# Asking for the next attention head's queries and keys a step sooner, in the middle of another chain of transfers

## The chip, the cores and the metric

One core of one Trainium2 chip runs the whole program. The metric is the device time of one execution in microseconds, the median of several runs. The engines are named as in the profile: PE multiplies matrices (PEld is its loading of weights), DVE works on vectors, ACT applies functions, POOL is the general engine and SP only issues transfers. Each engine works through its own list of instructions in order and waits at semaphores for the others. A DMA issued by SP is an instruction in SP's list too: it takes time there, and if it has to wait for something, all that SP has to issue after it waits as well.

## The reference

The program is a network of two layers on an image tensor of 4 x 32 x 32 x 384 values. The change lies in the attention of the first layer, per image 1024 tokens and 12 heads of width 32:

```python
qkv = x.reshape(B, N, C) @ qkv_w.T
attn = jax.nn.softmax(jnp.einsum('bhnd,bhmd->bhnm', q, k) * scale, axis=-1)
...                      # each query joins a group; each group picks its 96 best keys
row = gw.sum(axis=-1)
col = mask.sum(axis=2)   # how many groups of this head picked a key
attn = attn * (row[..., :, None] * col[..., None, :])
attn = attn / (attn.sum(axis=2, keepdims=True) + 1e-08)
out = jnp.einsum('bhnm,bhmd->bhnd', attn, v)
return out.transpose(0, 2, 1, 3).reshape(B, H, W, NH * HD) @ proj_w.T
```

Two normalisations follow each other: the softmax divides by a sum over the keys, and the second one divides by a sum over the queries of what the first has left. So the exponentials of a head must be there for all keys, and their sum over keys must be known for each query, before the second sum can be taken. After the attention come a mixture of experts, a local attention and a last feed-forward layer, which the change leaves alone.

## The kernel before, in words

The attention runs over 48 heads (4 images of 12) in 192 steps, four steps for each head. A step handles a pair of key blocks, 256 keys against all 1024 queries. Three heads are under way at once, and the loop at L889 writes out by hand what each step does, for head n = step // 4 and pair u = step % 4:

- `scores` (L649): PE multiplies keys by queries into `ps_s`. Four groups of 32 rows work side by side, so queries and keys of the head have first to be copied from the layout of the whole image (`q`, `k`: one tile for four heads) into `q4` and `k4`, each with 4 x 32 partitions. The copies are eight DMAs of 64 KB (L636 and L637, a q and a k for each r), issued by SP in the constructor of `Head`. There are two buffers of each.
- `exps` (L659): ACT takes the exponential of `ps_s` into `e`, with 17 buffers.
- `out` (L667, into `ps_o`): PE multiplies values by the weighed exponentials of a pair eight steps back, that is of head n-2. It needs `wv` of that pair. In PE's list it stands right behind the scores of the step.
- `total` (L667, into `ps_z`): PE sums the exponentials of the step before over the keys.
- `gather`, at u = 0, for head n-1, whose sums are now complete: ACT copies them to `zr` (L681); SP writes them to a row in memory (`z_row`, L683), waits for that to land and reads them back spread over the partitions (`zz`, L685).
- `keep`, at u = 3, for head n-2: ACT copies the head's result to `po`, and four DMAs bring it into the place of the head's queries, two from SP (L740) and two that accumulate from POOL (L738).
- `share` (L711 to L718), seven steps behind the scores, so first at u = 3 for head n-1: DVE multiplies the exponentials by `rz`, the reciprocals of the sums repeated on all partitions, sums over the queries as it goes, and makes `wv` from the values.
- `spread`, at u = 1, for head n-1: DVE adds the two halves of `zz` (`zall`, L693) and takes the reciprocal `rr` (L695); SP writes it to a row (`r_row`, L697), waits for its landing, and reads the row back to all partitions (`rz`, L699, 512 KB).

At the end of step u = 1 the loop makes `Head(n + 1)` (L933), with the eight loads, for scores that come three steps later. In SP's list they stand behind `r_row` and `rz`.

Other transfers go by SP between these. In steps 4 to 75 each step writes a block of zeros to memory (`room`, L85, called at L924). For 16 steps of each image but the first, tiles of the image before are projected: every second step stores a finished tile (L787), and the step after it loads the next tile's residue into the same buffer, so that the load waits for the store (L764). The tokens of the next image are fetched by L221.

PE has spare room in a step, which a planner fills with work for the next image, so much per step (`goal`, `spent`). Each piece has a cost and may have a condition. One condition, at L536, holds the making of a new chunk of `q` and `k` back until the head that reads the old chunk last has been made: `len(heads) > NH * (b - 1) + 4 * c + 3`.

Of the kernel before, what the change touches and what calls it, by code (L numbers as in the profile page):

```python
# [10 lines left out]
FP = mybir.dt.float32  # L11
# [6 lines left out]
P = 128  # L18
B, IMG, C = 4, 32, 384
NTOK = IMG * IMG  # L20
NB = NTOK // P
# [155 lines left out]
def attention(net, outer, router, x, x1, unsafe, qkv_wT, gpT, proj_wT, proj_w, gate_w, gate_b):  # L177
# [15 lines left out]
    NHEAD = B * NH  # L193
# [8 lines left out]
    with ExitStack() as ctx:  # L202
# [6 lines left out]
        tiny = ctx.enter_context(tc.tile_pool(name="at_tiny", bufs=4))  # L209
# [106 lines left out]
        def cost(time):  # L316
            nonlocal spent
            spent += time
# [6 lines left out]
        reached, heads, projected, valued = set(), [], set(), set()  # L325

        def rows_of(t):
            return min(P, ROWS - P * t)

        def load(b, t):  # L330

            im = images[b]
            n = rows_of(t)

            parts, r = [], 0
            while r < n:
                c, o = divmod(P * t + r, GW)
                w = min(n - r, GW - o)
                parts.append((c, o, r, w))
                r += w  # L340
            left = work.tile([P, NTOK], FP, name="tk_left", tag="tk_left", bufs=2)
            for half in range(2):
                cols = slice(half * 512, half * 512 + 512)
                ps = psum()
                for c, o, r, w in parts:
                    nc.tensor.matmul(
                        ps[r : r + w, :], lhsT=qmbd[:, c, o : o + w], rhs=im["k"][c][:, cols],
                        start=True, stop=True,
                    )
                nc.scalar.copy(left[:n, cols], ps[:n, :])  # L350
            loaded.add((b, t))
            cost(1.8 * len(parts))
            return left
# [267 lines left out]
        class Head:  # L621
            def __init__(self, n):
                self.n, self.b, self.h = n, n // NH, n % NH
                self.c, self.j = self.h // 4, self.h % 4
                self.rows = slice(32 * self.j, 32 * self.j + 32)
                self.im = images[self.b]
                assert (self.b, self.c, "qk") in reached

                self.q4 = big.tile([P, 512], FP, name="q4", tag="q4", bufs=2)
                self.k4 = big.tile([P, 512], FP, name="k4", tag="k4", bufs=2)  # L630
                q = self.im["q"][self.c][self.rows, :]
                k = self.im["k"][self.c][self.rows, :].rearrange("p (a e t) -> p a e t", e=2, t=P)
                for r in range(4):
                    rows_ = slice(32 * r, 32 * r + 32)
                    odd, half = divmod(r, 2)
                    nc.sync.dma_start(out=self.q4[rows_, :], in_=q[:, 512 * half : 512 * half + 512])  # L636
                    nc.sync.dma_start(  # L637
                        out=self.k4[rows_, :].rearrange("p (a t) -> p a t", t=P), in_=k[:, :, odd, :]
                    )
                self.es = []  # L640
                self.s = tiny.tile([P, NB], FP, name="s", tag="s")

            def scores(self, u):
                self.ps = []
# [30 lines left out]
                    self.z = ps_z.tile([P, 512], FP, name="ps_z", tag="z")  # L675
                self.four(self.z, u, lambda odd: ones)

            def gather(self):

                zr = work.tile([P, 512], FP, name="zr", tag="zr", bufs=1)  # L680
                nc.scalar.copy(zr, self.z)  # L681
                there = rows.tile([4, 512], FP, name="z_row", tag="z_row")
                nc.sync.dma_start(out=there, in_=zr.rearrange("(j r) q -> j r q", r=32)[:, 0, :])  # L683
                self.zz = tiny.tile([P, 2, NB], FP, name="zz", tag="zz", bufs=2)
                nc.sync.dma_start(  # L685
                    out=self.zz,
                    in_=there.rearrange("j q -> (j q)").rearrange("(e p i) -> p e i", e=2, p=P),
                )
# [68 lines left out]
        def residue(b, t):  # L757
            if late:
                o = late[0].tile([P, C], FP, name="o", tag="o", bufs=2)
            else:  # L760
                o = few.tile([P, C], FP, name="o", tag="o", bufs=1)
            residues[b, t] = o
            r = b * NTOK + t * P
            nc.sync.dma_start(out=o, in_=x[r : r + P, :])  # L764

        def project(b, t):
            im = images[b]
            r = b * NTOK + t * P
            if t == 0:
                im["o"] = few.tile([P, NB, NE], FP, name="gate_o", tag="gate_o", bufs=1)  # L770
                im["mv"] = few.tile([P, NB, 2], FP, name="mv", tag="mv")
            o = residues.pop((b, t))
            cost(2.0)
            ps = psum()
            linear(
                ps[:, : C + NE], lambda k: images[b]["q"][k][:, t * P : (t + 1) * P],
                lambda k: wproj[:, k, :],
            )
            projected.add((b, t))

            def add():
                nc.vector.tensor_tensor(o, o, ps[:, :C], ALU.add)
                nc.vector.tensor_copy(im["o"][:, t, :], ps[:, C : C + NE])
                st = few.tile([P, 6], FP, name="o_st", tag="o_st")
                nc.vector.bn_stats(st, o)
                nc.vector.bn_aggr(im["mv"][:, t, :], st)
                nc.sync.dma_start(out=x1[r : r + P, :], in_=o)  # L787

            ends.append(add)
# [56 lines left out]
        def search():  # L846

            for one in list(searching):
                if next(one, 0) == 0:
                    searching.remove(one)  # L850

        def widen(step):

            nonlocal begun
            if len(searching) < 2 and begun < len(tiles) and step >= begun * TURN - 9 and ready(*tiles[begun]):
                searching.append(topk(*tiles[begun]))
                begun += 1
                next(searching[-1])

        def begin(step):  # L860
            now[0] = step
            for f in others.pop(step, []):
                f()

        def end():
            while ends:
                ends.pop(0)()
# [8 lines left out]
        for step in range(-AHEAD, 0):  # L876
# [8 lines left out]
                search()  # L885
            end()
        heads.append(Head(0))
        goal = spent
        for step in range(STEPS + OUT + 2):  # L889
            n, u = divmod(step, PAIRS)  # L890
            if n < NHEAD:
                heads[n].scores(u)
            if n < NHEAD:
                heads[n].exps()
            if 0 <= step - OUT < STEPS:
                heads[(step - OUT) // PAIRS].out((step - OUT) % PAIRS)
            if 0 <= step - 1 < STEPS:
                heads[(step - 1) // PAIRS].total((step - 1) % PAIRS)
            if u == 0 and 0 < n <= NHEAD:
                heads[n - 1].gather()  # L900
            if 0 <= step - OUT < STEPS:
                if (step - OUT) % PAIRS == PAIRS - 1:
                    heads[(step - OUT) // PAIRS].keep()
            b, i = divmod(step, PAIRS * NH)
            goal = min(goal + (RAMP if step < 12 else PACE), spent + MOST)
            begin(step)
            if step < 12:
                search()
                search()
            widen(step)  # L910
            o, t = i - OUT - 2, (i - OUT - 2) // 2
            if b and 0 <= o < 2 * NB and o % 2 == 0:
                project(b - 1, t)
            if b and 0 <= o + 1 < 2 * NB and o % 2:
                residue(b - 1, t + 1)
            if b and o > 2 * NB:
                next(routing[b - 1], None)
            if b < B:
                for t in {3: [0], 4: [1, 2], 5: [3], 6: [4], 7: [5, 6], 8: [7]}.get(i, []):
                    value(b, t)  # L920
            while spent < goal and prepared():
                pass
            if zeros and step >= 4:
                zeros.pop(0)()  # L924
            if 0 <= step - SHARE < STEPS:
                heads[(step - SHARE) // PAIRS].share((step - SHARE) % PAIRS)
            if u == 1 and 0 < n <= NHEAD:
                heads[n - 1].spread()
            search()
            end()  # L930
            search()
            if u == 1 and n + 1 < NHEAD:
                heads.append(Head(n + 1))  # L933
        residue(B - 1, 0)
        assert not ends and not others
        assert pending == [None, None] and begun == len(tiles) and not searching and not zeros
# [1529 lines left out]
```

## Time and profile before

| | us |
|---|---|
| median of three runs (2771.51 to 2787.73) | 2778.27 |
| the profiled execution | 2779.0 |
| its span, first to last instruction | 2776.9 |
| PE, DVE, ACT, POOL busy in the span | 2563.9, 1746.2, 1272.1, 414.5 |
| attention's stretch, 75 to 1225 us: PE busy | 1017.1 |
| the same stretch: DVE, ACT busy | 824.2, 791.7 |
| the stretches after it: 1225 to 1980, 1980 to 2690, 2690 to 2777: PE busy | 741.7, 680.4, 75.0 |
| SP, one ask each, median: q<-q, k<-k | 0.597, 0.632 |
| SP, one ask each, median: zz<-z_row, rz<-r_row | 0.372, 0.320 |

A row of the list of waits reads: the engine and line that waited, what it waited for, then the microseconds in total, how often, and the longest. In a timeline a row gives the start, the duration and the instruction, with equal neighbours merged (x8), and in brackets the idle time of the engine before it with what ended it. "SPq" is SP's list: its rows are asks of DMAs, not the transfers. When a transfer has landed is seen from what waits for it.

### The profile page before, as it was taken

How to read it: one execution, taken by the hardware profiler on the slowest of the kernel's cores; microseconds unless marked ns; L12 is line 12 of the kernel's file. 1: busy time of each engine (PE TensorE's matmuls, PEld its weight loads, DVE VectorE, ACT ScalarE, POOL GpSimd, SP SyncE). 2: the span in 40 equal slices, each digit the busy share in tenths (PEclk: the TensorE clock that was granted, in tenths of full speed). 3: DMA queues.
4: the chain of work that ended last, by engine and by line, in shares of the span. 5: the costliest groups of instructions: out<-in, count | busy, mean ns of one | idle time of the engine just before them, and what ended most of it. 6: DMA issues, size and time to landing. Idle time of an engine off the chain costs nothing. (4 is left out here: it accounts for less than half of the span.)

```text
span 2776.9 us, 40200 instructions
## 1 busy us (share of the span) xinstructions
PE 2563.9 (92%) x14667; PEld 1555.7 (56%) x14667; DVE 1746.2 (63%) x4490; ACT 1272.1 (46%) x2086; POOL 414.5 (15%) x501
## 2 busy tenths in 40 slices
PE   6879998989898999679999999999999998999988
PEld 3323332333332332137889999999999974555542
DVE  2367768777776778555635444455465457897962
ACT  3768776667676777421121211211211123445455
POOL 1000000020003000412221111222222111110000
PEclk9989999989998999779999999999999999999999
DMA  5133334322331233445475455556656626765532
GB/s 108 33 98 91 103 91 124 104 56 63 92 78 46 70 87 85 130 128 190 158 280 207 181 187 207 213 208 222 228 195 223 225 100 220 213 213 180 174 117 93
DMA packets 215807, 404.13 MB, mean 146 GB/s; under 512 B 83345, under 2 KB 176849, under 8 KB 202545
## 3 DMA queue, kind: packets, MB, share of 16 engines
q0 software_dynamic: 26960, 209.05, 21.9%
q1 hardware_dynamic: 178928, 181.52, 21.8%
q10 hardware_dynamic: 9712, 10.91, 1.3%
q8 instruction: 118, 1.93, 0.3%
q14 instruction: 89, 0.72, 0.1%
HBM read 304.34 MB, written 49.00 MB: 127 GB/s over the span
## 5 line engine op out<-in xcount | busy, mean ns | idle before, releaser
L1728 ACT ACTIVATE h<-ps_h,up 128x256 f32<-128x256 f32 (+1 forms) x420 | 194.9, 465 | 835.2 <-PE ps_h L1723 818.6
L1723 PE MATMUL ps_h<-xbT,up 128*128 128x256 f32 (+1 forms) x2520 | 531.2, 371 | 2.5 <-ACT h L1728 1.4
L1723 PEld LDWEIGHTS ps_h<-xbT,up 128*128 128x128 f32 x2520 | 462.4, 191 | 64.9 <-ACT h L1728 2.2
L711 DVE CUSTOM_DVE_ANT_0 e<-e,rz,inv 128x1024 f32<-128x1024 f32 x384 | 475.2, 1274 | 35.7 <-DMA rz<-r_row 35.7
L659 ACT ACTIVATE e<-ps_s,ten 128x1024 f32<-128x1024 f32 x384 | 407.6, 1107 | 96.5 <-PE ps_s L649 41.6
L649 PE MATMUL ps_s<-q,k 32*128 32x512 f32 x1536 | 291.3, 669 | 66.1 <-ACT e L659 32.7
L667 PE MATMUL ps_o<-e,wv 128*32 128x512 f32 x1536 | 229.0, 671 | 47.6 <-DVE wv L718 30.2
L738 POOL DMA_DIRECT2D q<-po x96 | 76.0, 874 | 977.9 <-DMA q<-po 651.1
L667 PE MATMUL ps_z<-e,rt_ones 128*32 128x512 f32 x1536 | 219.7, 646 | 0.0
L391 ACT ACTIVATE below<-tk_left,tk_bound 128x1024 bf16<-128x1024 f32 (+1 forms) x160 | 184.2, 1151 | 70.6 <-DVE tk_bound L397 60.1
L1767 PE MATMUL ps_y<-wsum,hsum 128*128 128x192 f32 x1116 | 197.1, 330 | 9.9 <-DVE hsum L1683 5.4
L649 PEld LDWEIGHTS ps_s<-q,k 32*128 32x128 f32 x1536 | 89.4, 191 | 203.2 <-issue 89.3
L1767 PEld LDWEIGHTS ps_y<-wsum,hsum 128*128 128x128 f32 x1116 | 183.3, 192 | 13.7 <-DVE y L1771 7.4
L1907 PE MATMUL ps_a<-wa,xnT 128*128 128x486 f32 x384 | 162.4, 572 | 1.8 <-ACT xnT L174 1.8
L1771 DVE TENSOR_TENSOR y<-ps_y,y 128x192 f32<-128x192 f32 x155 | 55.4, 357 | 167.8 <-PE ps_y L1767 162.0
L667 PEld LDWEIGHTS ps_o<-e,wv 128*32 128x32 f32 x1536 | 31.7, 112 | 209.0 <-issue 83.5
L306 PE MATMUL ps_t<-xnT,wqkv 128*128 128x512 f32 x288 | 136.9, 616 | 3.3 <-ACT xnT L488 2.6
L1567 POOL DMA_INDIRECT yt<-yg,index x64 | 78.0, 1218 | 358.8 <-DVE x L1870 164.7
L667 PEld LDWEIGHTS ps_z<-e,rt_ones 128*32 128x32 f32 x1536 | 52.8, 118 | 132.7 <-issue 129.7
L1767 PE MATMUL ps_y<-down,h 128*128 128x192 f32 x744 | 126.0, 326 | 0.0
L1767 PEld LDWEIGHTS ps_y<-down,h 128*128 128x128 f32 x744 | 122.6, 190 | 1.6
L1907 PEld LDWEIGHTS ps_a<-wa,xnT 128*128 128x128 f32 x384 | 71.2, 189 | 74.2 <-issue 70.2
(403 smaller groups left out, 3588.1 us busy)
## 6 DMA issues: line engine op xcount, KB each, us to landing
band<-room SPq DMA_DIRECT2D x32, 1560.0 KB
rz<-r_row SPq DMA_DIRECT2D x48, 512.0 KB
yg<-y SPq DMA_DIRECT2D x67, 192.0 KB
q<-q SPq DMA_DIRECT2D x192, 64.0 KB
k<-k SPq DMA_DIRECT2D x192, 64.0 KB
room<-none SPq DMA_DIRECT2D x64, 192.0 KB
x<-x SPq DMA_DIRECT2D x34, 192.0 KB
o<-in_x_dram SPq DMA_DIRECT2D x33, 192.0 KB
```

The lines of the kernel that those rows point to most:

```text
L306: nc.tensor.matmul(ps, lhsT=lhsT(k), rhs=rhs(k), start=k == 0, stop=k == KC - 1)
L391: nc.scalar.activation(junk[:n], left[:n], AF.Sign, bias=bound[:n], accum_out=over[:n])
L649: nc.tensor.matmul(ps[:, half * 512 : half * 512 + 512], lhsT=self.k4[r, u * P : (u + 1) * P], rhs=self.q4[r, :], start=True, stop=True,)
L659: nc.scalar.activation(e, ps, AF.Exp, bias=shift, scale=QK_SCALE)
L667: nc.tensor.matmul(ps[r : r + 32, :], lhsT=lhsT(odd), rhs=self.es[2 * u + odd][:, half * 512 : half * 512 + 512], start=u == 0, stop=u == ...
L711: nc.vector.tensor_tensor_reduce(self.es[m], self.es[m], self.rz, 1.0, self.im["inv"][:, m, self.h : self.h + 1], ALU.mult, ALU.add, self. ...
L738: nc.gpsimd.dma_start(out=there, in_=po[r : r + 32, :], accum_op=ALU.add)
L1567: self.nc.gpsimd.indirect_dma_start(out=y, out_offset=None, in_=self.net.yg[: first_row(self.complete(i // NB)), :], in_offset=bass.Indire ...
L1723: nc.tensor.matmul(ps, lhsT=up[:, o : o + P], rhs=xbT[:, k, :size], start=k == 0, stop=k == KC - 1,)
L1728: nc.scalar.activation(hs[f // 3][:, f % 3, :size], ps, AF.Gelu, bias=up[:, KC * HID + f : KC * HID + f + 1])
L1767: nc.tensor.matmul(ps, lhsT=left[f], rhs=right[:, f, :], start=f == 0, stop=f == HF - 1)
L1907: nc.tensor.matmul(pa[:, :HW_], lhsT=xnTs[i][:, k, :], rhs=wa[:, k, hh * HW_ : (hh + 1) * HW_], start=k == 0, stop=k == KC - 1,)
```

## The change

`Head`'s constructor only makes the tiles; a generator `load` issues the eight DMAs, stopping after each. The head is made at u = 0 of the head before it, not at the end of u = 1. `gather` is given the generator and takes three of the loads between the ask of `z_row` and that of `zz`; the other five follow right behind `zz`. Head 0 is loaded in one go before the loop, head 1 at step 0.

```diff
@@ class Head
+                self.es = []
+                self.s = tiny.tile([P, NB], FP, name="s", tag="s")
+
+            def load(self):
+
                 q = self.im["q"][self.c][self.rows, :]
...
                     nc.sync.dma_start(out=self.q4[rows_, :], in_=q[:, 512 * half : 512 * half + 512])
+                    yield
                     nc.sync.dma_start(
                         out=self.k4[rows_, :].rearrange("p (a t) -> p a t", t=P), in_=k[:, :, odd, :]
                     )
-                self.es = []
-                self.s = tiny.tile([P, NB], FP, name="s", tag="s")
+                    yield
...
-            def gather(self):
+            def gather(self, loads):
...
                 nc.sync.dma_start(out=there, in_=zr.rearrange("(j r) q -> j r q", r=32)[:, 0, :])
+                for _ in range(3):
+                    next(loads, None)
                 self.zz = tiny.tile([P, 2, NB], FP, name="zz", tag="zz", bufs=2)
@@ the loop over steps
         heads.append(Head(0))
+        for _ in heads[0].load():
+            pass
...
-            if u == 0 and 0 < n <= NHEAD:
-                heads[n - 1].gather()
+            if u == 0 and n <= NHEAD:
+                loads = iter(())
+                if n + 1 < NHEAD:
+                    heads.append(Head(n + 1))
+                    loads = heads[-1].load()
+                if n:
+                    heads[n - 1].gather(loads)
+                for _ in loads:
+                    pass
...
-            if u == 1 and n + 1 < NHEAD:
-                heads.append(Head(n + 1))
```

The transfers are the same in number, size and shape.

## The prediction

> **What bounds the kernel now.** I read the table of stretches first: attention, 75 to 1225 us, is the stage with a slack engine clock and idle matrix time (PE busy 1017.1 of 1150 us; the four shorter stretches each show it), and the diff touches nothing outside it. What the change can win or lose there has to come out of PE's 133 idle us, so next came the list of waits for that window. Three rows name the two things that share the sync queue: a head's loads (first two lines) and the row of reciprocals that DVE needs before it may weigh the exponentials (last two).
>
> ```profile
> PE ps_s L649 <- DMA q<-q: 11.7, 1, 11.7
> PE ps_s L649 <- DMA k<-k: 11.0, 10, 4.2
> PE ps_o L667 <- DVE wv L718: 30.2, 14, 5.2
> DVE e L711 <- DMA rz<-r_row: 35.7, 15, 13.2
> ```
>
> Then the order of the queue itself, from the timeline of SP after head 7's sums are ready (columns: start, duration, what):
>
> ```profile
> 281.24 0.55 SPq L683 DMA_DIRECT2D z_row<-zr  x1
> 282.98 0.38 SPq L685 DMA_DIRECT2D zz<-z_row  x1
> 283.40 1.24 SPq L85 DMA_DIRECT2D room<-none  x2
> 285.07 0.32 SPq L697 DMA_DIRECT2D r_row<-rr  x1
> 286.57 0.33 SPq L699 DMA_DIRECT2D rz<-r_row  x1
> 287.36 0.59 SPq L636 DMA_DIRECT2D q<-q  x1
> 287.99 0.66 SPq L637 DMA_DIRECT2D k<-k  x1
> ...
> 291.97 0.63 SPq L637 DMA_DIRECT2D k<-k  x1
> ```
>
> Each ask waits for the landing of the one before it: z_row to zz 1.74 us, zz to r_row 2.1 us (landing, an add, a reciprocal), r_row to rz 1.5 us. The last of head 9's eight loads is asked at 292.60, and head 9's first scores (DVE and PE timelines) need it:
>
> ```profile
> 290.40 1.27 DVE L711 CUSTOM_DVE_ANT_0 e<-e,rz,inv 128x1024 f32<-128x1024 f32 x1
> 293.12 0.22 DVE L718 TENSOR_TENSOR wv<-v,d 128x64 f32<-128x64 f32 x1
> ```
>
> ```profile
> 292.40 1.53 PE L649 MATMUL ps_s<-q,k 32*128 32x512 f32 x6
> 294.13 1.09 PE L649 MATMUL ps_s<-q,k 32*128 32x512 f32 x2 [0.21 <-DMA k<-k]
> 295.16 1.06 PE L667 MATMUL ps_o<-e,wv 128*32 128x512 f32 x8
> ```
>
> The scores stretch to 2.8 us where other heads show 1.14. But ps_o of head 7 comes right behind them, and its weights wv were done only at 293.34. So PE has two late guests at this step, and they are nearly equally late. That is the heart of the case.
>
> **What the change gains.** For every head I compared the first ps_o behind its first scores with the earliest it could start with the loads already there: PE's previous end and ACT's last two exponentials, and wv of the head two back. The difference (loads' lateness not covered by wv) is 1.7 us at head 9, 0.7 at 10, 2.1 at 18, 2.3 at 28, 1.8 at 30, 0.9 at 42, 1.0 at 43, 1.6 at 47; elsewhere the loads end over 1 us ahead or something else binds. Sum: 12.1 us, if rz comes no later than now. The new asks begin right behind z_row, some 5 us sooner, and no first scores would wait for them: that part I take as certain but for head 47 (see below).
>
> **What the change costs: the sum's own asks.** The loads take SP's time: 0.60 us for q, 0.63 for k by the median of their rows, 0.66 from one ask to the next (287.36 to 291.97 is seven of them). Three now stand between z_row and zz, where 1.74−0.59 = 1.15 us were idle; five between zz and r_row, where some 1.7 to 1.8 were. Zz: 0.58 + 3×0.66 = 2.6 us behind z_row, not 1.74, so 0.8 later. Loads end at 2.6 + 0.42 + 5×0.66 = 6.3. A plain head's r_row then goes at 6.3, not 3.9: 2.4 us late, and rz, which nothing shortens, as late. Where the two room writes lie between (heads 4 to 10) they no longer fit in idle time: 6.3 + 2×0.62 = 7.6, so 3.8 late. Where a finished tile is stored and the next residue loaded (L787, L764; heads 14, 16, 28, 38 to 41), the residue waits for the store's landing and r_row stands behind it: at head 38 that is 6.3 + 1.35 + 1.5 + 0.4 = 9.6, where the timeline has 5.4: 4.2 late. Where r_row waited anyway for DVE or ACT (heads 1, 2, 11, 15, 26, 29, 44: it went 6 to 14 us behind z_row) nothing is lost.
>
> What is queued behind: on DVE the add that waits for zz, then the first weighing (L711) of that head and all DVE work after it; on PE the ps_o that needs wv, and everything behind; ACT's second exponential of that step, whose buffer that ps_o frees. POOL's accumulating writes (L738) hang on the asks of L740 two steps on, by when SP has caught up: nothing. Keeping the queue clear at the end of the old step costs nothing either way.
>
> Rz's lateness reaches PE only past two covers: DVE was busy elsewhere when rz landed, and wv was ready before PE came. Per head (r_row late − DVE's cover − PE's cover, with the worst of the four pairs):
> Head 4: 3.8−0.5−0.4 = 2.9, of which 1.5 falls into an idle wait of PE's that follows (ACT's g): 1.4. Head 7: 3.8−0−1.3 = 2.5. Head 8: 3.2−0.3−0.8 = 2.1, swallowed by the 3.4 us wait for ACT's exponential that follows: 0. Head 14: 4.0−0.3−1.0 = 2.7. Head 16: 3.8−0.2−2.1 = 1.5 (its store also queues behind a 768 KB load). Head 28: 3.5−0.3−1.8 = 1.4. Head 38: 4.2−0.5−0.6 = 3.1, less a 0.7 wait: 2.4. Head 39: 3.0−0.3−1.3 = 1.4. Head 40: 3.0−0.4−0.9 = 1.7. All others have cover: in plain heads 18 to 25, 30 to 37 and 42 to 43 the 2.4 us is met by 1.9 to 12 us of DVE and PE slack. Sum: 15.0 us lost.
>
> Now the gains again, since ps_o takes the later of its two guests. Heads 9, 10, 18, 30 and 42 have as second guest wv of heads 7, 8, 16, 28 and 40, which are in that list: their losses are counted from a ps_o that already waited for loads, so their gains are gone. Head 28 keeps 2.2 (head 26's r_row is hardly late), head 43 nothing (41 is 0.3 to 0.9 late), head 47 0.3: 2.5 us kept.
>
> **Net:** +15.0 − 2.5 = +12.5 us.
>
> **Unknown costs, from both sides.** (1) Zz and r_row now stand in the DMA rings behind loads. Behind nothing, zz lands in 1.65 us, r_row in 1.4. The Trainium skill (DMA: Bandwidth & Descriptors, Queues, rings and completion order) says that each DMA engine takes descriptors in ring order, which speaks against this change; what it costs depends on whether a backlog stands there. Head 9's last load fed a matmul 1.5 us after its ask had ended, as fast as the 8 KB zz: no backlog at one 64 KB load per 0.66 us. I take 0; by the rule with half a us on each, the same sum over heads rises by 5, with a full us by 12. Below nothing: rz of heads 46 and 47, with no loads asked behind, landed 3.3 to 3.4 us after its ask against about 3.55 for the rest; 0.2 on eight paying heads is −1.6.
> (2) The same page (Issuing engines are not separate DMA queues) says that the time a sequencer takes to start a DMA is usually small beside the DMA. By that rule the eight asks would push nothing and the sum would be −12.1. The row says 0.60 to 0.63 each, back to back, and z_row to zz is only 1.74: I go by the row. At 0.50 per ask the losses would halve, at 0.35 they vanish.
> (3) The planner asks `len(heads) >` before it makes a chunk of the next image's q and k; heads are listed two steps sooner. The copies into q and k show four chunks held by exactly this (steps 26, 42, 90, 138); they move two steps forward. The matmuls are the same; a step with them is 5.7 us, one without 3.3 to 4.0, of which PE works 3.3. Between −0.7×2×4 = −5 and, if they meet a DVE-bound step, +5. I take 0.
> (4) Head 47's loads and r_row meet the first expert weights: r_row took 10.3 us to land there. Loads asked sooner get ahead of part of that traffic, but r_row falls behind them: −2 to +3, taken as −0.3.
> Moving `es` and `s` in the constructor issues nothing: 0. Head 1's loads are asked at step 0 on an idle queue: 0.
>
> **The sum.** The profiled execution took 2779.0 us (span 2776.9 and 2.1 around it), 0.7 over the median of 2778.27. 2779.0 + 12.5 = 2791.5, against the median 2790.8: I say 2791.
>
> **Rivals.**
> *Late sums, as above*: 2784 to 2799, 47%. For it: ask times and the order of the queue, both measured. Against: each cover is one execution's.
> *Loads win* (faster): PE's wait for loads at its first scores goes, and rz comes in time. It decides from the point where r_row is under about 1 us late in the storing and room-writing heads, that is if an ask costs under 0.45 us or DVE is usually busy past rz's landing. Then 2779.0−12.1 = 2767; 18%. For it: 22.7 us of PE waits carry the loads' names. Against: 11.7 of these are one event at head 47 where DVE waited 13.2 for rz at the same time.
> *They cancel*, or the early scores let ACT run ahead so that PE catches up behind a late ps_o: within 5 of 2779; 17%.
> *Sums later still*: ring backlog of half to one us, or paying heads among those I covered: 12.5 + 5 to 12 and a few more heads, 2797 to 2810; 18%.
>
> The runs shown spread over 16 us, so about 0.5% (14 us) is what a measurement here can tell from no change. Faster than 2764: 10% (half of the second). Slower than 2792: nearly half of the first and all of the last, 42%. Same: 48%. For 8 in 10 the range goes from the second's middle to within the last: 2767 to 2806.
>
> **What would show it.** Right: in SP's timeline zz about 2.6 us behind z_row, r_row 6.3 to 9.6; no rows "PE ps_s L649 <- DMA"; "DVE e L711 <- DMA rz" up from 35.7 to over 55 us, "ps_o L667 <- wv" up by 10 or more, and zall's wait up. Wrong: asks at 0.35 us; r_row at 4 to 5; or rz late with no more wait of PE for wv, its cover then being larger than this trace has it.

## The result, and the profile after

The changed kernel takes 2818.52 us (median of six runs, 2812.01 to 2826.27); the kernel before, run beside it, 2777.74. The ratio is 1.0163, 95% interval 1.014 to 1.0186: 40.8 us slower, where the prediction said 12.5. The direction was right, the size was not, and 2818 lies above the range of 2767 to 2806.

The list of waits of the changed kernel over its attention (75 to 1272 us; the largest rows of VectorE and TensorE that bear on the change, some rows between them left out; columns: microseconds in all, times, longest) answers to the one before:

```profile
DVE e L718 <- DMA rz<-r_row: 75.9, 34, 5.6
DVE zall L700 <- DMA zz<-z_row: 71.2, 29, 17.2
PE ps_o L672 <- DVE wv L725: 50.2, 20, 11.4
PE ps_s L654 <- ACT e L664: 36.5, 26, 4.2
PE ps_o L672 <- DVE tk_parts L395: 36.3, 11, 8.2
...
PE ps_t L487 <- DVE gate_o L790: 8.2, 5, 3.0
```

The kernel before has for three of these, beside the rows already shown:

```profile
DVE zall L693 <- DMA zz<-z_row: 35.4, 19, 4.1
PE ps_o L667 <- DVE tk_parts L395: 13.7, 6, 3.9
PE ps_t L487 <- DVE gate_o L783: 2.3, 3, 1.3
```

In the change there is no row of scores that wait for a DMA any more: the loads are in time everywhere. VectorE's wait for rz has more than doubled (35.7 before), and so has its wait for zz. Two rows are the wait for the weights wv at the output sums: the one that says so (30.2 before), and the one put down to tk_parts, an operation that starts on VectorE right behind wv as wv ends. Together they went from 43.9 to 86.5 us. The last row is new in this size: matmuls between the steps wait for VectorE too.

SP's timeline of the changed kernel, first behind the sums of head 7 (the head of the prediction's timeline), then behind those of head 40, where a tile is stored and a residue loaded (columns: start, duration, what):

```profile
287.98 0.55 SPq L688 DMA_DIRECT2D z_row<-zr  x1
...
290.61 0.52 SPq L692 DMA_DIRECT2D zz<-z_row  x1
...
293.83 0.63 SPq L643 DMA_DIRECT2D k<-k  x1
294.84 1.37 SPq L85 DMA_DIRECT2D room<-none  x2
296.31 0.55 SPq L704 DMA_DIRECT2D r_row<-rr  x1
298.12 0.33 SPq L706 DMA_DIRECT2D rz<-r_row  x1
...
1090.11 0.63 SPq L643 DMA_DIRECT2D k<-k  x1
1090.85 0.53 SPq L794 DMA_DIRECT2D x<-o  x1
1092.99 0.34 SPq L771 DMA_DIRECT2D o<-in_x_dram  x1
1093.42 0.38 SPq L704 DMA_DIRECT2D r_row<-rr  x1
1095.60 0.32 SPq L706 DMA_DIRECT2D rz<-r_row  x1
```

From z_row to rz it takes 10.1 us at head 7, where it was 5.3. What becomes of this at head 40 is seen on VectorE and TensorE:

```profile
1096.69 0.18 DVE L793 BATCH_NORM_AGGREGATE mv<-o_st 128x2 f32<-128x6 f32 x1
1099.78 1.28 DVE L718 CUSTOM_DVE_ANT_0 e<-e,rz,inv 128x1024 f32<-128x1024 f32 x1 [2.91 <-DMA rz<-r_row]
...
1102.52 0.22 DVE L725 TENSOR_TENSOR wv<-v,d 128x64 f32<-128x64 f32 x1
```

```profile
1095.68 1.61 PE L654 MATMUL ps_s<-q,k 32*128 32x512 f32 x8
1102.89 1.94 PE L672 MATMUL ps_o<-e,wv 128*32 128x512 f32 x8 [5.60 <-DVE tk_parts L395]
1104.57 1.92 PE L672 MATMUL ps_z<-e,rt_ones 128*32 128x512 f32 x8
...
1108.57 1.14 PE L654 MATMUL ps_s<-q,k 32*128 32x512 f32 x8
```

Rz lands 4.2 us after its ask, wv is ready 3 us behind that, and TensorE has stood 5.6 us. Then a second thing shows: ps_o and ps_z take 1.9 us each, where 1.07 and 1.04 are usual. The granted clock is 0.50 from 1101 to 1104 us and full again from 1107. My prediction had no such term, so a theory of the cause had to include it.

**Where the time is.** The kernel before and the change were profiled once more on one chip (e8 and e7 below), and each stretch from the first scores to the last ps_o was split: TensorE's idle time, its busy time, and of this half of what it was busy while the granted clock was 0.5.

| us | before (e8) | change (e7) |
|---|---|---|
| TensorE's work, counted at full clock | 943.1 | 935.7 |
| added by half clock | 77.2 | 88.6 |
| idle | 124.1 | 166.5 |
| of it ahead of ps_o / ps_s / ps_t | 57.2 / 47.6 / 18.9 | 95.1 / 39.9 / 29.2 |
| the stretch | 1144.3 | 1190.8 |

So +46.5 us is 42.4 of waits, 11.4 of clock and −7.4 of work. Both stretches hold the same 6470 matmuls, so the −7.4 says how exact the last two terms are: TensorE's busy time as a whole rose by only 4.0 us. All that follows the stretch takes about the same (1545 and 1552 us).

### The profile page after: what moved, and what is told of

Same layout as the page of the kernel before. It is cut to its first block, busy times and chain, and to the rows that moved or that the text cites. A ratio compares the mean times of both kernels' runs of the same rounds, so it can differ in the third digit from the quotient of the medians.

```text
span 2817.5 us, 40166 instructions
## 1 busy us (share of the span) xinstructions
PE 2572.7 (91%) x14667; PEld 1555.7 (55%) x14667; DVE 1747.8 (62%) x4490; ACT 1273.5 (45%) x2086; POOL 415.3 (15%) x501
## 5 line engine op out<-in xcount | busy, mean ns | idle before, releaser
L718 DVE CUSTOM_DVE_ANT_0 e<-e,rz,inv 128x1024 f32<-128x1024 f32 x384 | 475.8, 1276 | 76.2 <-DMA rz<-r_row 75.9
L672 PE MATMUL ps_o<-e,wv 128*32 128x512 f32 x1536 | 237.6, 695 | 96.2 <-DVE wv L725 50.2
L654 PE MATMUL ps_s<-q,k 32*128 32x512 f32 x1536 | 280.5, 671 | 37.6 <-ACT e L664 36.5
L672 PE MATMUL ps_z<-e,rt_ones 128*32 128x512 f32 x1536 | 228.8, 670 | 0.0
L1781 PEld LDWEIGHTS ps_y<-wsum,hsum 128*128 128x128 f32 x1116 | 183.4, 192 | 12.5 <-DVE hsum L1697 6.7
```

Of the source, the lines that this page charges most:

```text
L654: nc.tensor.matmul(ps[:, half * 512 : half * 512 + 512], lhsT=self.k4[r, u * P : (u + 1) * P], rhs=self.q4[r, :], start=True, stop=True,)
L672: nc.tensor.matmul(ps[r : r + 32, :], lhsT=lhsT(odd), rhs=self.es[2 * u + odd][:, half * 512 : half * 512 + 512], start=u == 0, stop=u == ...
L718: nc.vector.tensor_tensor_reduce(self.es[m], self.es[m], self.rz, 1.0, self.im["inv"][:, m, self.h : self.h + 1], ALU.mult, ALU.add, self. ...
L1781: nc.tensor.matmul(ps, lhsT=left[f], rhs=right[:, f, :], start=f == 0, stop=f == HF - 1)
```

## The experiments

My theory: the eight asks ahead of r_row make rz late, ps_o waits, and each wait costs up to double because the clock falls (row theory, with the clock theory as its second half). Rivals: the planner, which the new position of the heads' list makes move work (in the change's trace four makings of q and k come two steps sooner, into steps that hold a head's first ps_o), and traffic, that the loads themselves get in the way of the small transfers, whoever asks for them. The kernel before took 2751 to 2752 us beside some of the runs and 2776 to 2782 beside others (chip 8 gave both: 2775.7 beside e5 to e8, 2752.3 beside e13 to e15), for no reason that the record shows; so ratios to the kernel before, run side by side, are compared, and microseconds only between runs made side by side. "Landing" is the median, over heads 3 to 43, of the time from the end of zr to the end of the last 4 KB packet of rz: 9.4 to 9.5 us in the kernel before, 13.3 in the change.

**e7, e8: the change and the kernel before once more, e16: the change on another chip.** No edit.

> The change itself once more, so that the other runs have it, with a profile, on their chip: 1.5 to 1.8% above the kernel before. Against the run with the planner held (1.0154): if the planner's shift carries nothing, the ratio is between 1.012 and 1.019; if it carries a good part of the loss, 1.02 or more.

> The kernel before, unchanged, for a profile on the same chip as the others. Clock theory: its stretch with attention holds at least 35 us less at half clock than the same stretch of the change beside it. If the half clock is a thing of the chip and not of the waits: within 15 us of it.

> The change itself, to set beside the two runs that follow on the same chip: 1.0155 to 1.021 of the kernel before.

1.0155 (1.0113 to 1.0198) and 1.0164 (1.0144 to 1.0183): the result stands on other chips too. Half clock in the stretch was 189.9 us before and 226.1 in the change, 36 more.

**e1: the planner held.**

```diff
-                    (b == 0 or len(heads) > NH * (b - 1) + 4 * c + 3)
+                    (b == 0 or asked() > NH * (b - 1) + 4 * c + 3)
...
+        def asked():
+            n, u = divmod(now[0], PAIRS)
+            return len(heads) - (now[0] >= 0 and u < 2 and n + 1 < NHEAD)
```

> The change, but the condition that frees a query and key chunk for preparing counts the next head only from the third step of a head, as in the kernel before; the order of asks on SP stays that of the change. Row theory (the late reciprocal row makes the output sums wait, and the waits halve TensorE's clock): most of the +40.8 us stays, 2803 to 2820. Planner theory (preparing work moved by two steps carries the loss): 2780 to 2797.

1.0154 (1.0134 to 1.0175). The microseconds of the expectation don't apply here (2796 beside 2751), the ratio does: the whole loss is there with the planner as before. The planner's rival falls; what it moves changes where the waits stand (78.9 us ahead of the first ps_o of a head, 56 to 66 in the change's runs), not their sum.

**e2, e12: GpSimd asks, with the planner held and as in the change.**

```diff
             def load(self):
...
-                    nc.sync.dma_start(out=self.q4[rows_, :], in_=q[:, 512 * half : 512 * half + 512])
+                    nc.gpsimd.dma_start(out=self.q4[rows_, :], in_=q[:, 512 * half : 512 * half + 512])
...              # the same for k4
```

> As the run with the planner held, but the eight loads of a head are asked by GpSimd in place of SP, so that they are as early as in the change and nothing stands between the finished head's asks. Row theory: the row rz lands as in the kernel before, and the loads' gain is left: 2765 to 2778. Traffic theory (the eight transfers themselves, early, get in the way of the small ones, whoever asks): 2795 to 2815.

> The change with nothing altered but the queue of the eight loads: GpSimd asks them, the planner is as in the change. Row theory: within 0.3% of the run with GpSimd's asks and the planner held (0.9948), so 0.992 to 0.998. If the planner's shift costs something that the late row hid: 1.000 or more.

0.9948 (0.9932 to 0.9965) and 0.9918 (0.9896 to 0.994): both faster than the kernel before. e12 differs from the change in nothing but who asks, and is 2.4% below it by the ratios. E12's SP timeline at head 7 and its waits:

```profile
279.74 0.54 SPq L688 DMA_DIRECT2D z_row<-zr  x1
281.86 0.37 SPq L692 DMA_DIRECT2D zz<-z_row  x1
282.28 1.24 SPq L85 DMA_DIRECT2D room<-none  x2
284.03 0.33 SPq L704 DMA_DIRECT2D r_row<-rr  x1
285.44 0.33 SPq L706 DMA_DIRECT2D rz<-r_row  x1
```

```profile
PE ps_o L672 <- DVE wv L725: 40.4, 19, 6.0
...
DVE e L718 <- DMA rz<-r_row: 27.9, 11, 10.2
...
PE ps_o L672 <- DVE tk_parts L395: 17.5, 8, 4.1
```

The row is nearly as quick as before (5.7 us from z_row to rz, 5.3 there), rz's wait is back at 27.9, and the loads' transfers, still early, are in no one's way. Traffic falls. The first half of the row theory holds: it is the asks on SP that make rz late.

**e14: GpSimd asks, at the old place.** The kernel before, with the same edit of its two asks.

> The kernel before, with the eight loads at their old place asked by GpSimd in place of SP. If the 0.5 to 0.8% that the early loads asked by GpSimd gain comes from their being early: 0.997 to 1.002. If it comes from SP being freed of 384 asks: 0.990 to 0.996.

0.9963 (0.995 to 0.9976), between the two cases of the expectation. But the run doesn't part them as meant: by the traces GpSimd asked a head's first load 25.1 us ahead of its first scores (median), exactly as in e2 (the kernel before 10.1, the change some 16.6). One line of its waits says why:

```profile
POOL q L636 <- PE ps_s L649: 563.0, 40, 54.1
```

GpSimd has little to do and waits for the buffer, that is for the last scores that read it; the place in the program doesn't matter. So e2, e12 and e14 all do two things at once: the loads are early, and SP is free of its 384 asks.

**e18: on SP, ahead of z_row.** The head is made and its loads asked behind the last scores of the head two before it, whose buffers they take; planner held.

```diff
                 heads[n].exps()
+            if len(heads) < NHEAD and (step == 0 or u == PAIRS - 1):
+                heads.append(Head(len(heads)))
+                for _ in heads[-1].load():
+                    pass
```

> The eight loads stay on SP, asked behind the last scores of a head, ahead of the finished head's z_row in place of behind it (planner held). By the traces the buffers come free some 8 us before the finished head's sums are copied, and the eight asks take 5.3 us, so nothing is late. Chain theory: zz, r_row and rz as in the kernel before, loads 8 us sooner than in the change: 0.990 to 0.998. Rival (SP's other work then, the stores of a finished head and the residue, is pushed back and holds the projections, or z_row is late anyway): 1.003 or more.

SP's timeline of e18 around the sums of head 7:

```profile
274.03 0.63 SPq L647 DMA_DIRECT2D k<-k  x1
274.79 1.17 SPq L749 DMA_DIRECT2D q<-po  x2
...
278.02 0.54 SPq L692 DMA_DIRECT2D z_row<-zr  x1
279.75 0.37 SPq L694 DMA_DIRECT2D zz<-z_row  x1
...
283.35 0.33 SPq L708 DMA_DIRECT2D rz<-r_row  x1
```

0.9991 (0.9978 to 1.0004): 48.9 us below the change on the same chip (e16), landing 9.4, zz and rz where the kernel before has them. It isn't SP, it is the place. But against the kernel before nothing is gained that stands clear of the noise, though the loads are earliest of all (26.7 us ahead of the scores); the expectation missed that by 0.1%. TensorE's idle time in e18 is 29.5 us ahead of the scores and 76.6 ahead of ps_o; in e8, which was not run beside it, 47.6 and 57.2. So the waits seem to have moved more than gone.

**e5: all eight behind zz; e3: spread over SP's waits; e15: half the asks.** e5 takes out the three `next(loads, None)` ahead of zz. e3 (planner held) puts one load behind z_row, two behind zz, two between r_row and rz, three behind rz. In e15 GpSimd asks for the queries, SP for the keys.

> The change, with all eight loads behind zz in place of three ahead of it: zz is asked as early as in the kernel before (about 1.7 us behind z_row), r_row still stands behind ten asks. Queue theory (what counts is how many asks stand ahead of r_row on SP, some 6.6 us of them, wherever they stand): within 5 us of the change run beside it. Theory that the late zz itself hurts (VectorE stands at its sum of zz, and the work behind it on VectorE with it): 8 to 20 us below the change.

> Planner held; the eight loads are put where SP waits anyway: one behind z_row, two behind zz, two between r_row and rz, three behind rz. Row theory: rz is late by 1 us at most, loads are 5 us earlier than in the kernel before: 2766 to 2780. Planner theory: the same as the run with the planner held. Traffic theory: 2795 to 2815, as with GpSimd's asks.

> The change, with the four loads of queries asked by GpSimd and the four of keys by SP: one ask stands ahead of zz and three behind it, ahead of r_row. Chain theory: SP has room for about these four while it waits for z_row and for VectorE, so rz is late by 1 us at most: 0.993 to 1.001. If the loss went with the number of asks, half of the way between the two: 1.002 to 1.005. If it is the early keys that hurt, whoever asks for the queries: 1.010 or more.

e5: 1.0216 (1.0176 to 1.0256), 10.9 us above the change beside it, outside both theories. Its SP timeline at head 7:

```profile
288.71 0.55 SPq L688 DMA_DIRECT2D z_row<-zr  x1
290.45 0.38 SPq L690 DMA_DIRECT2D zz<-z_row  x1
290.88 0.53 SPq L641 DMA_DIRECT2D q<-q  x1
...
297.85 0.32 SPq L702 DMA_DIRECT2D r_row<-rr  x1
301.55 0.33 SPq L704 DMA_DIRECT2D rz<-r_row  x1
```

SP stands idle from 289.26 to 290.45, where the change asks for loads, and r_row is later still: landing 14.4. My arithmetic had forgotten this idle time. The mechanism is the queue theory's: had the late zz hurt, this run would have been the faster one. e3: 1.0044 (1.003 to 1.0059), above its expectation; e15: 1.0028 (1.0014 to 1.0042), its second case. In both rz lands at 10.8, 1.3 later than before, not the 1 or less that I had hoped for. Together they make a dose:

| run | landing, us | ratio |
|---|---|---|
| e18 / e2 / e12 | 9.4 / 9.6 / 9.5 | 0.9991 / 0.9948 / 0.9918 |
| e15 / e3 | 10.8 / 10.8 | 1.0028 / 1.0044 |
| e1 / e16 / e7 | 13.4 / 13.3 / 13.3 | 1.0154 / 1.0164 / 1.0155 |
| e5 | 14.4 | 1.0216 |

With early loads the time follows the landing of rz: from the mean of the first row (0.9952) to that of the third (1.0158) it rises by 0.54% or 15 us for each microsecond, a third of the 48 that it would be if no head had any cover. The 0.3 to 0.4% of e15 and e3 against the kernel before lie clear of the noise too: four or five asks ahead of rz still cost something.

**e4: asked twice.** e1, with the same eight loads asked again at their place of before, so that scores wait for the late ones.

> Planner held; the loads are asked early as in the change, and once more (the same values) at their place of before, so that the scores wait for the late ones. The asks between the sums stay, the gain of early loads goes. Row theory: 5 to 15 us above the run with the planner held, 2812 to 2832 (the waits of the scores for loads of before, some 12 us, come back in part). If the early loads gave nothing: equal to it. Planner theory: 2780 to 2797.

1.0286 (1.0263 to 1.0309), 33.5 us above e1 where I had said 5 to 15.

```profile
DVE e L722 <- DMA rz<-r_row: 91.8, 33, 15.6
PE ps_s L658 <- DMA k<-k: 50.0, 18, 12.9
...
PE ps_o L676 <- DVE wv L729: 33.7, 16, 5.3
...
PE ps_o L676 <- DVE tk_parts L395: 10.1, 5, 3.2
```

Rz is as late as in e1 (landing 13.4), yet ps_o waits 47 us, not 106: TensorE now stands at the scores, 75 us, and comes to ps_o late as well. Only one of two late guests is seen in a list of waits. It is no clean price of early loads, since the second asks stand behind the late rz and land later than before.

**e6, e11, e13, e17: the waits filled.** Matmuls that no one reads (the real sums overwrite them) ahead of the first ps_o of the heads that wait: 80, 45 (42 in the expectation was a miscount), 25 and again 25.

```diff
                     self.po = ps_o.tile([P, 512], FP, name="ps_o", tag="o")
+                    for _ in range(FILL.get(self.n, 0)):
+                        nc.tensor.matmul(
+                            self.po, lhsT=wqkv[:, 0, :P], rhs=wqkv[:, 0, :512], start=True, stop=True,
+                            skip_group_check=True,
+                        )
```

> The change, with 3 to 14 matmuls more (no one reads what they write; the output sums overwrite it) ahead of the first output sums of twelve heads at which TensorE waits by the trace of the change, so that it isn't idle there. Clock theory (each wait of 3 us or more is followed by 3.4 to 7 us at half clock, so that it costs up to twice its length): 12 to 30 us below the change, though work was added. Wait theory (only the wait itself costs): equal to the change or up to 5 us above it.

> The change, with matmuls that no one reads ahead of the first output sums of thirteen heads, this time 1 to 7 of them, sized by 0.86 us each to end within the waits (42 in all, 36 us). Clock theory: nothing is pushed out, the half clock falls by 40 us or more, and the time falls by half of what TensorE was busy in it, 10 to 25 us below the change. Wait theory: within 5 us of the change.

> The change, with matmuls that no one reads ahead of the first output sums of twelve heads, 25 in all (some 24 us), each group at least 0.6 us shorter than the wait that it fills. Clock theory: the half clock falls by 25 us or more and the time by 8 to 15 us, ratio 1.010 to 1.0125. Chain theory (at these heads the end is set by the reciprocal row's way through SP, DMA and VectorE, and TensorE has time to spare): within 4 us of the change, 1.014 to 1.0175.

> The change with the 25 small fills of the earlier run, beside the change on one chip. Clock theory: 8 to 15 us below the change. Chain theory: within 4 us of it.

What the fill does to the clock is plain in e11 at head 40: ps_o and ps_z are back at 1.06 and 1.04.

```profile
1098.81 5.42 PE L736 MATMUL ps_o<-wqkv 128*128 128x512 f32 x12
1105.24 1.06 PE L674 MATMUL ps_o<-e,wv 128*32 128x512 f32 x8 [1.01 <-DVE wv L727]
1106.12 1.04 PE L674 MATMUL ps_z<-e,rt_ones 128*32 128x512 f32 x8
```

But the time doesn't follow. e6 took 7.6 us more than e7 beside it, with 150 us at half clock in place of 226; e11 1.0154 (1.0137 to 1.0172), the ratio of the change, with 177; e13 1.0228 (1.0197 to 1.0259) without the change beside it, so e17 beside e16: 1.0203 (1.0185 to 1.0222), 8.1 us more, with 180 in place of 215. Not one of the four runs was faster. In e17 the fills lay inside the waits as meant (each of the twelve heads still waited behind its fill): TensorE's idle time ahead of ps_o fell from 95.6 us (e16) to 72.2, for 24.7 us of added matmuls. But the half clock's addition to TensorE's work fell only from 79.8 to 75.2 us, and the idle time ahead of the scores rose from 31.2 to 41.9, most of it waits for ScalarE's exponentials (30.7 to 39.6). The second half of my theory falls as far as these fills can tell: none recovered time by holding the clock up.

A likely reason is in the chain that ends the attention. Here it is followed back from the last ps_o, each piece to what released it (us, by kind of piece):

```
                            TensorE  VectorE  ScalarE   DMA  SP's asks
before (e8)                   654.8    205.0    123.0   97.3   19.2
change (e7)                   495.1    256.6    126.0  172.2   73.4   of it the loads' asks 58.7
change, waits filled (e11)    437.1    261.8    148.8  192.5   72.4
GpSimd asks (e12)             599.5    224.9    123.0  120.0    1.3
```

In the change 160 us of TensorE have left the chain; in their place stand the asks of the loads, the three small transfers and VectorE's weighing, that is the way from one head's sums to the next head's ps_o. Where that way sets the end, a TensorE kept at full clock has nothing to hurry for. This is a reading of the chain, which still holds 437 to 495 us of TensorE; no run tested it apart.

**e10, e9: ps_z ahead of ps_o** in each step, in the change and in e12.

> The change, with ps_z ahead of ps_o in each step: 0.9 us of slack more at each head. Slack theory: of the some 20 waits at the first output sums of a head about 0.9 us each goes, 15 to 25 us below the change, ratio 1.006 to 1.011. Rival (the waits end at work of VectorE that starts later too): within 6 us of the change, 1.0135 to 1.018.

> The loads asked by GpSimd, and the sums of the exponentials (ps_z) computed ahead of the output sums (ps_o) in each step, so that ps_o is reached 0.9 us later with nothing lost. Slack theory (a wait at ps_o is what the reciprocal row lacks of the slack of its head, so slack and lateness trade one for one): 10 to 20 us below the plain version with GpSimd's asks. If VectorE is so far behind that ps_z only moves the wait: within 4 us of it.

1.0195 (1.0154 to 1.0235) and 0.995 (0.9935 to 0.9966): neither gained (e9 took 7.1 us more than e12 beside it). The waits ahead of a head's first ps_o fell as the slack theory says (from 56.4 to 31.8 us against e7, from 35.7 to 22.3 against e12), but TensorE's work at full clock grew by 28 us in both (935.7 to 964.3, 936.4 to 964.7). What that growth is stays open; no run was made for it.

The best version run is e12, 0.9918 of the kernel before.

## Why the prediction was wrong in size

- **Asks and order: right.** Zz was predicted 2.6 us behind the sums and is at 2.6; r_row at 6.3 in plain heads, 7.6 with room writes, 9.6 at a store: 6.6, 8.4 (head 7) and 9.6 (head 40). The signs named for the waits came: no scores wait for loads, rz 75.9, wv up by 20.
- **Unknown (1), the rings, taken as 0: too low.** R_row to rz takes 1.86 us behind loads, 1.42 without (medians of e7 and e8), and the asks of zz and r_row themselves 0.58 and 0.53 in place of 0.37 and 0.33. With this, rz lands 2.8 us late in the median plain head (e8 to e7), where I had 2.4. The rule on ring order from the Trainium skill (DMA: Bandwidth & Descriptors, Queues, rings and completion order), which I set aside for want of a backlog, spoke in the right direction; that ring order is what slows the row no run shows.
- **Unknown (2), what an ask costs: right.** By the skill's sentence that starting a DMA is "usually small relative to the DMA itself" (same page, Issuing engines are not separate DMA queues), who asks would hardly matter; e12 against the change makes it 2.4%.
- **The gain of early loads, 12.1 us: not shown.** With rz in time and the loads early on SP, e18 gained 0.1%, 1.3 us, with an interval that holds zero. E2, e12 and e14 gained 0.4 to 0.8%, but SP was also free of the asks there. What early loads alone are worth stays open.
- **"Sum: 15.0 us lost": this step failed.** The same loads with and without the late row are e1 against e2, 58.3 us, and e16 against e18, 48.9 us. In both pairs the loads of the second are also earlier. The lateness itself was nearly right: for the nine heads that I had listed I had r_row late by 32.3 us in sum, and rz landed 35.3 later from e8 to e7. What failed is the cover, above all the sentence "All others have cover". From e8 to e7 the first scores of head 47 moved by 48.4 us; those nine heads account for 21 of it (counted over the four steps from the scores ahead of their first ps_o: 4, 38 and 40 lost 5.6 to 7.1 each where I had 1.4 to 2.4, heads 14 and 28 nothing); 27 came elsewhere. Heads 10, 25, 37, 41, 42 and 43, to which I had given cover, wait 1.2 to 3.1 us more at ps_o. I had set each head's lateness against the idle time of one trace, as if it ended there; but what stands behind it on VectorE is late too (gate_o rows ahead of TensorE's other work, 2.3 to 8.9 us from e8 to e7). That the head's own sums then go out late too, so that the next row starts late, fits the chain above, but no run shows it apart. Of a microsecond of lateness a third came through, by the dose table; my sum let a tenth through (15.0 over 48 heads at some 3 us).
- **Gains kept, 2.5 us.** Here the swap was seen rightly: the scores that stand ahead of the first ps_o of heads 8, 16 and 40 took 3.14, 4.37 and 3.06 us in e8 and 2.20, 1.62 and 1.61 in e7, and TensorE waits at ps_o in their stead, 3.1, 6.3 and 5.4 us.
- **Unknown (3), the planner, taken as 0: right** within the noise (e1; e2 and e12, not run side by side, leave 0.3% open).
- **The clock** was not in the sum. It is in the split (+11.4 us of 46.5, or less: busy time rose by 4.0), but no run in which fills raised the clock was faster.
- The rival "sums later still" had the mechanism and 18%; its upper end, 2810, was still 8 us short.

## What to carry to other kernels

An ask costs its queue's time whether or not its transfer is urgent: before moving asks ahead of a chain of small dependent transfers, count the idle time in that chain. Of what was tried here, asks ahead of the chain's first transfer (e18) or from a queue that isn't part of the chain (e12) left it alone; asks spread over its gaps (e3) or half as many (e15) still cost 0.3 to 0.4%. When a row that every iteration needs comes later, don't pay each iteration's lateness from the slack of one trace; follow the chain back from the end of the stage and see whether the row's own way is about to become the loop that sets the pace. Filling an engine's waits to keep its clock up won nothing here in four runs: see first whether the engine is what the end waits for.

## What the runs showed of the hardware

- From one to the next, asks of 64 KB took 0.65 to 0.68 us on SP (0.60 to 0.63 for the ask itself) and 0.55 on GpSimd, which asked as soon as the buffer came free.
- Small asks behind eight loads took longer to issue (0.33 to 0.53 us for r_row) and r_row to land (1.42 to 1.86 from its ask to that of rz, 0.2 of it the longer ask).
- The granted clock in the stretch was 0.5 or 1.0 only, and the spells of 0.5 came in multiples of 3.4 us, most of them behind a TensorE wait of 2.2 us or more (30 of 39 in e7); the Trainium skill (TensorE: Matmul & The Clock Gate, Part 1: The HAM clock gate) has the same 3.4 us. That a spell doubles the matmuls behind it (1.07 to 1.94 us) and that yet none of the fills won time back, I had not expected.
- The kernel before took 2751 to 2752 us beside some runs and 2776 to 2782 beside others, 1% apart and both on chip 8, so a difference of this size can be read only between runs made side by side.
